# A ternary feed-forward written as a pipeline over tiles, with its weights and first rows made beside the cross-attention ahead of it, and the head of the last attention cut into pieces

## The chip, the cores and the metric

The kernel runs on one core of one Trainium2 chip. Its metric is the time of one execution on the device, in microseconds (us), as a median over runs. A core has five engines with a queue of instructions each: TensorE (PE in the profile, with its weight loads as PEld), VectorE (DVE), ScalarE (ACT), GpSimd (POOL) and SyncE (SP), which here only issues DMAs. Each queue runs in order; queues wait for each other by semaphores.

## What is computed

A decoder of four layers on 16 sequences of 128 tokens with 256 features. Each layer has a mixer (`attn`), a cross-attention (`xattn`) on a context of 16 x 128 tokens with 192 features, and a feed-forward (`ffn`), each on the layer-normed rows and added to `x`. Two of the twelve blocks are rewritten by the change. Layer 1's feed-forward has ternary weights and rows rounded to 8 bits:

```python
def _weight_quant(w):
    scale = 1.0 / jnp.clip(jnp.mean(jnp.abs(w)), 1e-05)
    wq = jnp.clip(jnp.round(w * scale), -1.0, 1.0) / scale
...
def _act_quant(x):
    scale = 127.0 / jnp.clip(jnp.max(jnp.abs(x), axis=-1, keepdims=True), 1e-05)
    xq = jnp.clip(jnp.round(x * scale), -128.0, 127.0) / scale
...
gate = jax.nn.silu(_bitlinear(x, w_gate))
up = _bitlinear(x, w_up)
return _bitlinear(gate * up, w_down)
```

`w_gate` and `w_up` take 256 features to 1024, `w_down` takes them back. Layer 3's attention has 16 heads of 16 features, and each head attends over all 2048 tokens at once:

```python
flat = jnp.transpose(proj.reshape(B, S, H, hd), (2, 0, 1, 3)).reshape(H, B * S, hd)
q = jnp.einsum('hnd,hde->hne', flat, wq)
k = jnp.einsum('hnd,hde->hne', flat, wk)
logits = jnp.einsum('hne,hme->hnm', q, k) / jnp.sqrt(jnp.asarray(D, x.dtype))
attn = jax.nn.softmax(logits, axis=-1)
out = jnp.einsum('hnm,hmd->hnd', attn, flat)
```

## The kernel before

`x` stays on the chip: four groups (NG) of four tiles (GB) of 128 tokens (P), so a group has 512 tokens (GT) and there are 16 tiles (B). The blocks follow each other; a scheduler orders what is written in the program on each engine, by what is ready and within the buffers of the pools, except for TensorE instructions written as `pinned`, which keep their written order among themselves. Weights are fetched by `self.load` into a ring of seven large buffers (tag `w8`), so that a load is issued on SP's queue when an earlier weight's last reader is done.

*Cross-attention* (`xattn64`, L919). It is written as a pipeline over 32 units in layer 1: unit m is four head pairs of one tile of tokens. In each unit TensorE makes the sums of the unit before, scores, values of the unit before, the exponentials' shift, the row maxima of the unit after, and the projection of two units before. VectorE makes a reciprocal `r`, the product `cT`, the negated maxima `nm` and the addition to `x`. Once in four units a `prologue` makes keys, queries and values for the next four, evacuated by VectorE.

*Ternary feed-forward* (`l1_ffn`, L1099). VectorE first takes the absolute sums of the three weights (128 x 2048 each), then scales and clips them (L1122, L1123) and converts them to bf16 -1, 0, 1 (L1125). Then, group by group: layernorm and row rounding, both on GpSimd (L205, L1095), transposes `hTb`; and, tile by tile in halves of 512 columns: `gu` (gate and up together in PSUM, L166), Silu on ACT into `gy` (L1146), a scaled copy `up` on ACT (L1148), their product on GpSimd (L1149); then per tile the maximum (L1090), scale and rounding (L1095) on VectorE, `dy` on GpSimd (L1152), eight transposes `ytr` (L1158), `yT` on ACT (L1159), eight matmuls `down`, and the addition to `x` (L1165). Rounding is by adding and taking away a large constant, MAGIC.

*Last attention* (`l3_attn`). All matmul operands are split into bf16 parts that are summed in one matmul of 113 rows. The head makes, for each group, projections (`project`), the token-major values (`by_token`), and for each half of the features the parts of queries and keys (`split`), made by turns on ACT (L1886, L1892), POOL (L1889, L1893) and DVE (L1891), and written to memory; `fetch` brings them back, arranged by rows, as `qp` and `kp`. Row 112 of `qp` holds each query's negated maximum: `maxima` is a generator that makes one pair of score matmuls (`one`) and two reductions (L1978) at a time, 16 pairs for two heads and a group of queries; `some(n)` makes n pairs; `shift()` transposes finished maxima and sends them through memory into row 112 by two DMAs on POOL's queue (`shifts<-shift`, then `qp<-shifts`). The loop then runs 264 steps, each with two score matmul pairs `st`, exponentials (L2101), values `acc`, and two pairs of maxima for what comes later. In every 32nd step the fetches for a following window are issued, all at once:

```python
w, o = divmod(s - 8, 2 * B)
if o == 0 and 1 <= w and w + 1 < 8:
    queries(w + 1)
    if w % 2 == 0 and w // 2 + 1 < 4:
        keys(w // 2 + 1)
```

Of the kernel before, what the change touches and what calls it, by code (L numbers as in the profile page):

```python
# [8 lines left out]
F = mybir.dt.float32  # L9
BF = mybir.dt.bfloat16  # L10
U32 = mybir.dt.uint32
AF = mybir.ActivationFunctionType
ALU = mybir.AluOpType
# [16 lines left out]
class Decoder:  # L30
# [888 lines left out]
    def xattn64(self, H, names, bias, tag):  # L919
# [5 lines left out]
        wq, wo = self.load(names[0]), self.load(names[3])  # L925
        wk_, wv = self.load(names[1]), self.load(names[2])
        for w, n in ((wk_, names[1]), (wv, names[2])):
            nc.sync.dma_start(out=w[64:P, 1, :], in_=self.a[n][P:DC, :])
        R = lambda j: slice(64 * j, 64 * j + 64)
        S = lambda t: slice(t * P, (t + 1) * P)  # L930
        units = [(g, n, t) for g in range(NG) for n in range(H // 8) for t in range(GB)]
        with self.tc.tile_pool(name=tag, bufs=1) as wk:
# [132 lines left out]
            for m in range(N + 2):  # L1065
# [14 lines left out]
                if m < N and t == GB - 2 and m + 2 < N:  # L1080
                    state[(m + 2) // GB] = prologue(*units[m + 2][:2])

    def l1_xattn(self):
        self.xattn64(16, [f"L1_xattn_{n}" for n in ("Wq", "Wk", "Wv", "Wo")], "L1_xattn_bo", "l1x")

    def quantized(self, src, out, unit, engine):

        nc = self.nc
        nt = src.shape[1]
        nc.vector.tensor_reduce(unit, src, AX.X, ALU.max, apply_absolute_value=True)  # L1090
        nc.vector.tensor_scalar(unit, unit, 1e-5, 1.0 / 127.0, ALU.max, ALU.mult)
        q = self.small([P, nt], "qscale")
        nc.vector.reciprocal(q, unit)
        for t in range(nt):
            engine.tensor_scalar(out[:, t, :], src[:, t, :], q[:, t : t + 1], MAGIC, ALU.mult, ALU.add)  # L1095

    def l1_ffn(self):

        nc = self.nc  # L1099
        ws = [self.load(f"L1_ffn_{n}") for n in ("w_gate", "w_up", "w_down")]  # L1100
        with self.tc.tile_pool(name="l1f", bufs=1) as wk:

            mean = wk.tile([P, 3], F, tag="mean", name="mean")
            part = wk.tile([P, 3], F, tag="part", name="part")
            wsc = wk.tile([P, 3], F, tag="wsc", name="wsc")
            shift = wk.tile([P, 1], F, tag="shift", name="shift")
            nc.gpsimd.memset(shift, -MAGIC)
            for i, w in enumerate(ws):
                flat = w.rearrange("p c n -> p (c n)")
                p16 = self.small([P, 16], "p16")  # L1110
                nc.vector.tensor_reduce(
                    p16, flat.rearrange("p (a n) -> p a n", a=16), AX.X, ALU.add, apply_absolute_value=True
                )
                nc.vector.tensor_reduce(part[:, i : i + 1], p16, AX.X, ALU.add)
            ps = self.b1("wsum")[:, 0:3]
            self.mm(ps, [(self.ones, part)])
            nc.vector.tensor_scalar(mean, ps, 1.0 / (1024 * DM), 1e-5, ALU.mult, ALU.max)
            nc.vector.reciprocal(wsc, mean)
            wb = []
            for i, w in enumerate(ws):  # L1120
                flat = w.rearrange("p c n -> p (c n)")
                nc.vector.tensor_scalar(flat, flat, wsc[:, i : i + 1], 1.0, ALU.mult, ALU.min)  # L1122
                nc.vector.tensor_scalar(flat, flat, -1.0, MAGIC, ALU.max, ALU.add)  # L1123
                t = wk.tile(list(w.shape), BF, tag=f"wb{i}", name=f"wb{i}")
                nc.vector.tensor_scalar(t.rearrange("p c n -> p (c n)"), flat, -MAGIC, None, ALU.add)  # L1125
                wb.append(t)
            wg, wu, wd = wb
            for g in range(NG):
                h = self.layernorm(g, nc.gpsimd)
                ds = self.small([P, GB], "ds")  # L1130
                self.quantized(h, h, ds, nc.gpsimd)
                hT = wk.tile([P, 2, GT], BF, tag="hTb", name="hTb", bufs=2)
                self.transpose_group(h, hT, shift=-MAGIC)
                sg = self.small([P, 2, GB], "sg")
                for i in range(2):
                    nc.vector.tensor_scalar(sg[:, i, :], ds, mean[:, i : i + 1], None, ALU.mult)
                for t in range(GB):
                    y = wk.tile([P, 1, 1024], F, tag="gy", name="gy", bufs=3)
                    for n in range(2):
                        o = slice(n * 512, (n + 1) * 512)  # L1140
                        ps = self.b2("gu")
                        for i, w in enumerate((wg, wu)):
                            self.mm(
                                ps[:, i * 512 : (i + 1) * 512], [(hT[:, k, t * P : (t + 1) * P], w[:, k, o]) for k in range(2)]
                            )
                        nc.scalar.activation(y[:, 0, o], ps[:, 0:512], AF.Silu, scale=sg[:, 0, t : t + 1])  # L1146
                        up = wk.tile([P, 512], F, tag="up", name="up", bufs=2)
                        nc.scalar.activation(up, ps[:, 512:1024], AF.Copy, scale=sg[:, 1, t : t + 1])  # L1148
                        nc.gpsimd.tensor_tensor(y[:, 0, o], y[:, 0, o], up, ALU.mult)  # L1149
                    dy = self.small([P, 1], "dy")  # L1150
                    self.quantized(y, y, dy, nc.vector)
                    nc.gpsimd.tensor_scalar(dy, dy, mean[:, 2:3], None, ALU.mult)  # L1152
                    yT = wk.tile([P, 8, P], BF, tag="yT", name="yT", bufs=2)
                    for n in range(2):
                        ps = self.b1("ytr")
                        for k in range(4):
                            o = (4 * n + k) * P
                            nc.tensor.transpose(ps[:, k * P : (k + 1) * P], y[:, 0, o : o + P], self.ident)  # L1158
                        nc.scalar.activation(  # L1159
                            yT[:, 4 * n : 4 * n + 4, :].rearrange("p c n -> p (c n)"), ps, AF.Identity, bias=shift  # L1160
                        )
                    po = self.b1("down")[:, 0:DM]
                    self.mm(po, [(yT[:, k, :], wd[:, k, :]) for k in range(8)])
                    xt = self.x[g][:, t, :]
                    nc.vector.scalar_tensor_tensor(xt, po, dy[:, 0:1], xt, ALU.mult, ALU.add)  # L1165
# [647 lines left out]
    def l3_attn(self):  # L1813
# [40 lines left out]
        with self.tc.tile_pool(name="l3a", bufs=1) as wk:  # L1854
# [22 lines left out]
            def split(g, half):  # L1877

                ps = two("qk")
                for i in range(2):  # L1880
                    pinned(ps[:, i, :], wqk[:, i, half, :], pT[half][:, G(g)], start=True, stop=True)
                room = es[(g + half) % 3]
# [11 lines left out]
                for n in range(3):  # L1894
# [4 lines left out]
                    )  # L1899

            def transposed(g):
# [7 lines left out]
                return hT  # L1909

            def project(g, hT):
                ps = two("pT")
                for half in range(2):
# [4 lines left out]
                    )  # L1918

            def by_token(g):  # L1920
                for half in range(2):
# [5 lines left out]
                    )  # L1927

            def fetch(i, hg, dst, lo, n, want):

                for b in range(7):
                    j = 0
                    while j < 4:
                        m = j + 1
                        if want(b, j):
                            s = orders[j][i][b]
                            while m < 4 and want(b, m) and orders[m][i][b] == s:
                                m += 1
                            src = parts[s, i, (4 * hg + j) * 16 : (4 * hg + m) * 16, lo : lo + n]
                            moved(  # L1940
                                nc.sync, out=dst[16 * b : 16 * b + 16, j:m, :], in_=src.rearrange("(j r) n -> r j n", r=16)
                            )
                        j = m

# [5 lines left out]
            def queries(w, want=every):  # L1950

                fetch(0, w // 2, qp[w % 2], w % 2 * 2 * GT, 2 * GT, want)

            def keys(hg, want=every):
                fetch(1, hg, kp[hg % 2], 0, T, want)
# [55 lines left out]
            hT = transposed(0)  # L2011
            for g in range(NG):
                project(g, hT)
                if g + 1 < NG:
                    hT = transposed(g + 1)
                split(g, 0)
                by_token(g)
                if g < 2:
                    fetch(0, 0, qp[0][:, :, G(g)], g * GT, GT, first)
                fetch(1, 0, kp[0][:, :, G(g)], g * GT, GT, first)  # L2020
                if g > 0:
                    some(4)
                    fetch(1, 0, kp[0][:, :, G(g - 1)], (g - 1) * GT, GT, front)
                if g == 1:
                    fetch(0, 0, qp[0][:, :, G(0)], 0, GT, front)
            fetch(1, 0, kp[0][:, :, G(3)], 3 * GT, GT, front)
            split(0, 1)
            some(2)
            keys(0, back)
            split(1, 1)  # L2030
            some(2)
            fetch(0, 0, qp[0][:, :, G(1)], GT, GT, front)
            queries(0, back)
            split(2, 1)
            shift()
            some(3)
            split(3, 1)
            some(7)
            queries(1)
            keys(1)  # L2040

            def values(work):
# [243 lines left out]
```

## Time and profile before

| what | us |
|---|---|
| median of 3 runs | 3717.78 |
| their lowest and highest | 3717.32 and 3721.62 |
| profiled execution | 3721.63 |
| its span | 3719.9 |
| layer 1's cross-attention, in the span | about 1268 to 1639 |
| layer 1's feed-forward | about 1637.5 to 1769 |
| head of layer 3's attention | about 2551 to 2637.6 |
| its loop | 2637.6 to about 3380 |

The span runs from the first to the last instruction; the 1.7 us around it belong to the execution. A busy time counts an engine's instructions, not its waits. "PEclk" in the page and in the tables of stretches is the clock that TensorE was granted, as a share of full speed; over the whole span it was 0.941. Row by row, a group of instructions shows line, engine, operation, output and inputs, shapes and count, then the busy time and the mean of one in ns, then the idle time of that engine just ahead, with what ended it.

### The profile page before, as it was taken

Reading aid. Unit: us, or ns where it says so; the run is one execution under the profiler, and the core shown is the slowest. Engines: PE = TensorE matmul, PEld = TensorE weight load, DVE = VectorE, ACT = ScalarE, POOL = GpSimd, SP = SyncE. Lnnn points to the kernel's source line nnn. Section 1 sums busy time; section 2 is a strip of 40 time slices with the busy share of each in tenths; the row PEclk is TensorE's granted clock in tenths of the full one; section 3 lists DMA queues with packets and bytes.
Section 4 is the critical chain, followed back from the end, with each engine's and each line's share of the span. In section 5 each row is a group of like instructions: output and inputs, shape, how many; then the busy total and the mean of one; then the engine's idle time right before and its main releaser. Section 6 shows DMA issues by size and latency. Waiting matters only on the chain.

```text
span 3719.9 us, 51499 instructions
## 1 busy us (share of the span) xinstructions
PE 3379.5 (91%) x20976; PEld 1816.7 (49%) x20976; DVE 2095.8 (56%) x4102; ACT 1433.7 (39%) x1951; POOL 537.3 (14%) x690
## 2 busy tenths in 40 slices
PE   7888999999998899986799999386899999999999
PEld 4555655555556566653355556253122222224665
DVE  5545444444554444455577744424798999973440
ACT  2344311111124322236455522022476777774221
POOL 5423000000003211135000020102200000002100
PEclk9988999999999999998899999597799999999989
DMA  3000000000010100010000000282512020000000
GB/s 96 6 5 5 13 18 22 17 22 17 27 47 2 37 1 1 1 46 1 13 1 1 14 1 7 86 286 67 104 22 31 11 31 11 11 1 25 1 8 17
DMA packets 90486, 105.47 MB, mean 28 GB/s; under 512 B 11364, under 2 KB 72679, under 8 KB 89991
## 3 DMA queue, kind: packets, MB, share of 16 engines
q1 hardware_dynamic: 79672, 89.71, 9.3%
q0 software_dynamic: 4224, 6.43, 0.5%
q10 hardware_dynamic: 6352, 6.03, 0.5%
q8 instruction: 165, 2.70, 0.3%
q14 instruction: 73, 0.59, 0.1%
HBM read 85.53 MB, written 16.60 MB: 27 GB/s over the span
## 4 chain that ended last, share of the span: by engine, by line
PE 80%; DVE 9%; ACT 4%; POOL 3%; issue 3%; DMA 1%; SPq 0%; POOLq 0%; ACTq 0%; DVEq 0%
PE acc L1846 7%; PE down L255 6%; PE gate L255 6%; PE up L255 6%; PE st L1846 6%; PE proj L255 6%; PE one L1846 4%; PE st L255 4%; PE qT L166 3%; PE o L255 2%; PE h L255 2%; PE rb L255 2%; PE v L948 2%; PE pr L166 2%; PE kT L948 2%
## 5 line engine op out<-in xcount | busy, mean ns | idle before, releaser
L1978 DVE TENSOR_REDUCE mx<-one 128x1 f32<-128x512 f32 x1024 | 659.9, 686 | 54.1 <-PE one L1846 43.7
L2101 ACT ACTIVATE e<-st 128x1024 f32<-128x1024 f32 x512 | 496.9, 1021 | 210.8 <-PE st L1846 209.6
L674 ACT ACTIVATE gs<-gate,cols 128x512 f32<-128x512 f32 x132 | 90.8, 688 | 552.8 <-PE gate L255 552.7
L1846 PE MATMUL acc<-e,v 128*32 128x512 f32 x2048 | 290.5, 619 | 1.7 <-ACT e L2101 1.7
L1846 PE MATMUL st<-qp,kp 113*128 113x512 bf16 x1024 | 275.1, 389 | 10.0 <-ACT e L2101 5.7
L688 DVE SCALAR_TENSOR_TENSOR x<-down,w_all,x 128x256 f32<-128x256 f32 x512 | 212.3, 477 | 111.1 <-PE down L255 110.9
L255 PE MATMUL down<-expert,gs 128*128 128x256 f32 x1056 | 250.9, 381 | 2.2 <-DVE gs L675 2.2
L255 PE MATMUL gate<-hT,expert 128*128 128x512 f32 x528 | 250.3, 597 | 0.0
L255 PE MATMUL up<-hT,expert 128*128 128x512 f32 x528 | 248.8, 593 | 0.0
L255 PEld LDWEIGHTS down<-expert,gs 128*128 128x128 f32 x1056 | 201.4, 191 | 86.0 <-issue 61.5
L1846 PE MATMUL one<-kp,qp 16*128 16x512 bf16 x1024 | 224.5, 395 | 13.2 <-DVE mx L1978 7.5
L675 DVE SCALAR_TENSOR_TENSOR gs<-up,cols,gs 128x512 f32<-128x512 f32 x132 | 99.0, 750 | 230.1 <-PE up L255 230.0
L1846 PEld LDWEIGHTS <-qp 16*128 16x128 bf16 x1024 | 49.4, 91 | 333.9 <-issue 330.3
L255 PEld LDWEIGHTS up<-hT,expert 128*128 128x128 f32 x528 | 100.8, 191 | 127.2 <-issue 127.0
L1846 PEld LDWEIGHTS <-kp 113*128 113x128 bf16 x1024 | 79.4, 98 | 149.7 <-issue 87.9
L1050 DVE TENSOR_TENSOR cT<-o,rb 128x512 f32<-128x512 f32 x64 | 44.3, 692 | 165.2 <-ACT rb L1048 165.2
L1048 ACT COPY rb<-rb 128x512 f32<-128x512 f32 x64 | 37.5, 586 | 252.6 <-PE rb L255 252.6
L255 PEld LDWEIGHTS gate<-hT,expert 128*128 128x128 f32 x528 | 100.4, 192 | 70.5 <-issue 64.1
L166 PE MATMUL qT<-hT,L_xattn_Wq 128*128 128x512 f32 x256 | 116.4, 608 | 8.6 <-DVE hT L110 4.4
L1249 DVE SCALAR_TENSOR_TENSOR xs<-xBC,cols,xs 128x508 f32<-128x508 f32 x144 | 106.1, 741 | 22.2 <-ACT xs L1245 18.8
L255 PE MATMUL o<-e,v 128*32 128x128 f32 (+1 forms) x2048 | 105.7, 280 | 11.8 <-DVE nm L292 11.8
L780 POOL MEMSET v<- 128x256 f32 x16 | 5.4, 346 | 680.3 <-DVE bnmv L202 636.6
(516 smaller groups left out, 5643.0 us busy)
## 6 DMA issues: line engine op xcount, KB each, us to landing
W<-in_L_ffn_W_dram SPq DMA_DIRECT2D x46, 512.0 KB, 5.3
expert<-in_L_ffn_Wg_dram SPq DMA_DIRECT2D x32, 128.0 KB, 2.2
expert<-in_L_ffn_Wu_dram SPq DMA_DIRECT2D x32, 128.0 KB, 2.4
expert<-in_L_ffn_Wd_dram SPq DMA_DIRECT2D x32, 128.0 KB, 2.4
parts<-parts SPq DMA_DIRECT2D x16, 256.0 KB, 3.4
qp<-parts SPq DMA_DIRECT2D x28, 128.0 KB, 4.3
kp<-parts SPq DMA_DIRECT2D x12, 256.0 KB, 7.8
hs<-zero SPq DMA_DIRECT2D x23, 128.0 KB, 1.9
```

What stands on the lines that cost most here:

```text
L166: self.nc.tensor.matmul(out, lhsT, rhs, start=i == 0, stop=i == n - 1 and bias is None)
L255: self.tc.keep_in_program_order(self.nc.tensor.matmul(*a, **k))
L674: nc.scalar.activation(gs, pg, AF.Silu, bias=bg)
L675: nc.vector.scalar_tensor_tensor(gs, pu, bu, gs, ALU.add, ALU.mult)
L688: nc.vector.scalar_tensor_tensor(xt, pd[:, t, :], w_all[:, o : o + 1], xt, ALU.mult, ALU.add)
L948: nc.tensor.matmul(ps, l, r, start=True, stop=False)
L1048: nc.scalar.copy(rb, ps)
L1050: nc.vector.tensor_tensor(cT, po, rb, ALU.mult)
L1249: stt = lambda *a: pin(nc.vector.scalar_tensor_tensor(*a))
L1846: self.tc.keep_in_program_order(nc.tensor.matmul(*a, **k))
L1978: nc.vector.tensor_reduce(mx[:, t, kc, i : i + 1], pair[i], AX.X, ALU.max)
L2101: nc.scalar.activation(e[:, 2 * p : 2 * p + 2, :], ps, AF.Exp, scale=1.0 / 16.0)
```

## The change

1. `xattn64` takes a `begin` function; layer 1's hands back pieces of work by unit, which are written behind that unit's own work: absolute sums of the three weights at units 10 to 12, means at 13, scaling at 14 to 16, rounding at 17 to 19, layernorm statistics of groups 0 and 1 at 23 and of group 2 at 27, rounded rows at 24, 25 and 29, transposes at 27, 28 and 31, conversion to bf16 at 28 into buffers of the ring `w8`. All rows are made on VectorE. The order of weight loads changes to Wq, Wk, Wv, Wo in the cross-attentions of layers 1 to 3 that use `xattn64`.
2. `l1_ffn` is a loop over tiles with all TensorE instructions pinned: in step s the gate product of tile s, `down` of tile s - 3, the up product of tile s, the transposes of tile s - 2. Silu and the rounding run over 1024 columns at once on ACT, gate times up is one VectorE instruction that reads PSUM, and `dy` alone remains on GpSimd. Statistics, rows and transposes of group 3 stand in steps 1, 3 and 5.
3. In the head of the last attention the pieces of `split`, `project`, `transposed` and `by_token` are generators with a pair of maxima between them; `shift()` stands behind `split(1, 1)` rather than `split(2, 1)`; 27 pairs stand ahead of the loop rather than 26.
4. In its loop fetches are collected in a list and issued two in each step.

The functions that it replaces are printed above; the diff is cut to what is new.

```diff
-    def xattn64(self, H, names, bias, tag):
+    def xattn64(self, H, names, bias, tag, begin=None):
...
-        wq, wo = self.load(names[0]), self.load(names[3])
-        wk_, wv = self.load(names[1]), self.load(names[2])
+        wq, wk_, wv, wo = (self.load(n) for n in names)
         for w, n in ((wk_, names[1]), (wv, names[2])):
             nc.sync.dma_start(out=w[64:P, 1, :], in_=self.a[n][P:DC, :])
+        beside = begin() if begin else {}
...
+                for work in beside.get(m, ()):
+                    work()
...
+        self.xattn64(16, [f"L1_xattn_{n}" for n in ("Wq", "Wk", "Wv", "Wo")], "L1_xattn_bo", "l1x", self.l1_ffn_begin)
...
-    def l1_ffn(self):
...
+    def l1_ffn_begin(self):
...
+        def scaled(i):
+            nc.vector.tensor_scalar(flats[i], flats[i], wsc[:, i : i + 1], 1.0, ALU.mult, ALU.min)
+        def rounded(i):
+            nc.vector.tensor_scalar(flats[i], flats[i], -1.0, MAGIC, ALU.max, ALU.add)
+        def ternary():
+            t = self.wp.tile([P, 4, 1024], BF, tag="w8", name="gu8", bufs=7)
+            u = self.wp.tile([P, 8, DM], BF, tag="w8", name="down8", bufs=7)
+            st["w"] = t[:, 0:2, :], t[:, 2:4, :], u
+            for w, flat in zip(st["w"], flats):
+                nc.vector.tensor_scalar(w.rearrange("p c n -> p (c n)"), flat, -MAGIC, None, ALU.add)
...
+        def rows(g):
+            mv, rs = hs[g]
+            h = self.hp.tile([P, GB, DM], F, tag="h", name="h", bufs=2)
+            for t in range(GB):
+                nc.vector.tensor_scalar(
+                    h[:, t, :], self.x[g][:, t, :], mv[:, t, 0:1], rs[:, t : t + 1], ALU.subtract, ALU.mult
+                )
+            ds = self.small([P, GB], "l1ds")
+            q = self.scale8(h, ds, "l1q")
+            for t in range(GB):
+                nc.vector.tensor_scalar(h[:, t, :], h[:, t, :], q[:, t : t + 1], MAGIC, ALU.mult, ALU.add)
+            sg = self.small([P, 2, GB], "l1sg")
+            for i in range(2):
+                nc.vector.tensor_scalar(sg[:, i, :], ds, mean[:, i : i + 1], None, ALU.mult)
+            st["sg"][g] = sg
+            hs[g] = h
+        def turn(g):
+            if g % 2 == 0:
+                st["hT"].append(self.hp.tile([P, 2, 2, GT], BF, tag="hT", name="hTb", bufs=5))
+            for k in range(2):
+                ps = self.b1("tr")
+                for t in range(GB):
+                    self.pinned_transpose(ps[:, t * P : (t + 1) * P], hs[g][:, t, k * P : (k + 1) * P])
+                nc.vector.tensor_scalar(st["hT"][g // 2][:, g % 2, k, :], ps, -MAGIC, None, ALU.add)
+        st["last"] = [lambda: stats([3]), lambda: rows(3), lambda: turn(3)]
+        at = lambda f, *a: lambda: f(*a)
+        return {
+            10: [at(absolute, 0)],
+            11: [at(absolute, 1)],
+            12: [at(absolute, 2)],
+            13: [means],
+            **{14 + i: [at(scaled, i)] for i in range(3)},
+            **{17 + i: [at(rounded, i)] for i in range(3)},
+            23: [at(stats, [0, 1])],
+            24: [at(rows, 0)],
+            25: [at(rows, 1)],
+            27: [at(stats, [2]), at(turn, 0)],
+            28: [ternary, at(turn, 1)],
+            29: [at(rows, 2)],
+            31: [at(turn, 2)],
+        }
...
+    def l1_ffn(self):
...
+            def product(w, s):
+                g, t = divmod(s, GB)
+                ps = self.b2("gu")
+                hT = f["hT"][g // 2][:, g % 2]
+                for n in range(2):
+                    o = slice(n * 512, (n + 1) * 512)
+                    for k in range(2):
+                        self.pinned(ps[:, o], hT[:, k, t * P : (t + 1) * P], w[:, k, o], start=k == 0, stop=k == 1)
+                return ps
+            def gated(s, ps):
+                y = wk.tile([P, 1, 1024], F, tag="gy", name="gy", bufs=4)
+                nc.scalar.activation(y[:, 0, :], ps, AF.Silu, scale=f["sg"][s // GB][:, 0, s % GB : s % GB + 1])
+                return y
+            def quantized(s, y, ps):
+                sg = f["sg"][s // GB][:, 1, s % GB : s % GB + 1]
+                nc.vector.scalar_tensor_tensor(y[:, 0, :], ps, sg, y[:, 0, :], ALU.mult, ALU.mult)
+                dy = self.small([P, 1], "dy")
+                q = self.scale8(y, dy, "qy")
+                nc.gpsimd.tensor_scalar(dy, dy, f["mean"][:, 2:3], None, ALU.mult)
+                return dy, q
+            def turned(y):
+                yT = wk.tile([P, 8, P], BF, tag="yT", name="yT", bufs=3)
+                for n in range(2):
+                    ps = self.b1("ytr")
+                    for k in range(4):
+                        o = (4 * n + k) * P
+                        self.pinned_transpose(ps[:, k * P : (k + 1) * P], y[:, 0, o : o + P])
+                    nc.scalar.activation(
+                        yT[:, 4 * n : 4 * n + 4, :].rearrange("p c n -> p (c n)"), ps, AF.Identity, bias=f["down"]
+                    )
+                return yT
+            def down(s, yT, dy):
+                ps = self.b1("down")[:, 0:DM]
+                for k in range(8):
+                    self.pinned(ps, yT[:, k, :], wd[:, k, :], start=k == 0, stop=k == 7)
+                xt = self.x[s // GB][:, s % GB, :]
+                nc.vector.scalar_tensor_tensor(xt, ps, dy[:, 0:1], xt, ALU.mult, ALU.add)
+            ys, dys, yTs = {}, {}, {}
+            for s in range(B + 3):
+                if s < B:
+                    y = gated(s, product(wg, s))
+                if 0 < s <= B:
+                    z = ys[s - 1]
+                    nc.scalar.activation(z[:, 0, :], z[:, 0, :], AF.Identity, scale=qs, bias=f["up"])
+                if s > 2:
+                    down(s - 3, yTs.pop(s - 3), dys.pop(s - 3))
+                if s < B:
+                    ys[s] = y
+                    dys[s], qs = quantized(s, y, product(wu, s))
+                if 1 < s < B + 2:
+                    yTs[s - 2] = turned(ys.pop(s - 2))
+                if s in (1, 3, 5):
+                    f["last"][s // 2]()
...
                     pinned(ps[:, i, :], wqk[:, i, half, :], pT[half][:, G(g)], start=True, stop=True)
+                    if i == 0:
+                        yield
...
+            def issue(moves, n=99):
+                for out, in_ in moves[0:n]:
+                    moved(nc.sync, out=out, in_=in_)
+                del moves[0:n]
...
-            hT = transposed(0)
...
-            split(2, 1)
+            def first_keys(g):
+                issue(fetch(1, 0, kp[0][:, :, G(g)], g * GT, GT, first))
+            def run(pieces, pairs=0):
+                for _ in pieces:
+                    some(min(pairs, 1))
+            run(transposed(0))
+            for g in range(2):
+                run(project(g))
+                run(transposed(g + 1))
+                run(split(g, 0))
+                run(by_token(g))
+                issue(fetch(0, 0, qp[0][:, :, G(g)], g * GT, GT, first))
+                first_keys(g)
+            run(project(2), 1)
+            issue(fetch(1, 0, kp[0][:, :, G(0)], 0, GT, front))
+            run(transposed(3), 1)
+            run(split(2, 0), 1)
+            first_keys(2)
+            issue(fetch(0, 0, qp[0][:, :, G(0)], 0, GT, front))
+            run(by_token(2))
+            run(project(3), 1)
+            issue(fetch(1, 0, kp[0][:, :, G(1)], GT, GT, front))
+            run(split(3, 0), 1)
+            first_keys(3)
+            run(by_token(3), 1)
+            for g in (2, 3):
+                issue(fetch(1, 0, kp[0][:, :, G(g)], g * GT, GT, front))
+            run(split(0, 1), 1)
+            some(1)
+            issue(keys(0, back))
+            run(split(1, 1), 1)
+            issue(fetch(0, 0, qp[0][:, :, G(1)], GT, GT, front))
             shift()
-            some(3)
-            split(3, 1)
-            some(7)
-            queries(1)
-            keys(1)
+            some(1)
+            issue(queries(0, back))
+            run(split(2, 1), 1)
+            some(1)
+            run(split(3, 1), 1)
+            some(5)
+            waiting = queries(1) + keys(1)
...
-                    queries(w + 1)
+                    waiting += queries(w + 1)
                     if w % 2 == 0 and w // 2 + 1 < 4:
-                        keys(w // 2 + 1)
+                        waiting += keys(w // 2 + 1)
+                issue(waiting, 2)
```

## The prediction

> **What bounds the kernel now.** I read the totals and slices of the page first, then tables of busy time by stage, then the costliest groups, waits and chain inside the two stages that the change rewrites.
>
> ```profile
> PE 3379.5 (91%) x20976; PEld 1816.7 (49%) x20976; DVE 2095.8 (56%) x4102; ACT 1433.7 (39%) x1951; POOL 537.3 (14%) x690
> PE   7888999999998899986799999386899999999999
> PEclk9988999999999999998899999597799999999989
> ...
> 1522.00:1568.00 46.00, 45.47 (x376) 28.61 (x375) 19.34 (x31) 9.98 (x15) 11.29 (x16) 1.00 0.00 1
> ...
> 1640.00:1655.00 15.00, 5.03 (x18) 2.10 (x19) 14.68 (x21) 1.40 (x2) 12.12 (x4) 0.58 0.48 158
> 1655.00:1768.00 113.00, 76.14 (x401) 44.88 (x400) 63.43 (x150) 73.72 (x118) 61.55 (x60) 0.86 0.00 1
> ```
>
> TensorE is full nearly everywhere, so only its thin places can pay. Columns of the windows: stretch, its length, busy PE, PEld, DVE, ACT, POOL, granted clock, DMA share, GB/s. In the cross-attention (1522 to 1568) PE is 99% busy and DVE 42%. The ternary feed-forward (1637.5 to 1769, 131.5 us) begins with 15 us in which PE waits for VectorE to make the weights, then no engine is over 67% in 113 us: a chain passing from engine to engine.
>
> ```profile
> L1149 POOL TENSOR_TENSOR gy<-gy,up 128x512 f32<-128x512 f32 x32 | 40.8, 1292 | 22.8 <-ACT up L1148 19.8 <-PE down L166 3.0
> L1090 DVE TENSOR_REDUCE dy<-gy 128x1 f32<-128x1024 f32 x16 | 19.5, 1219 | 24.4 <-POOL gy L1149 24.4
> L205 POOL TENSOR_SCALAR h<-x,bnmv,rstd 128x256 f32<-128x256 f32 x8 | 17.0, 2134 | 6.6 <-PE tr L183 6.6
> ```
>
> The chain is GpSimd's: `gy` then `dy`, on one queue. `h` on the same queue adds whole blocks (the chain of waits shows one of 4.88 us at 1681.47).
>
> The last attention's head (2551 to 2637.6) is thin as well:
>
> ```profile
> 2592.00:2609.00 17.00, 14.25 (x30) 5.45 (x30) 6.48 (x11) 4.41 (x6) 3.97 (x5) 0.70 0.37 113
> 2609.00:2638.00 29.00, 22.24 (x48) 5.33 (x48) 18.76 (x32) 11.82 (x13) 18.82 (x12) 0.74 0.72 181
> ...
> 2862.68 0.53 POOL L1852 DMA_DIRECT2D qp<-shifts  x1 [8.13 <-PE st L1846]
> 2866.89 1.04 PE L1846 MATMUL st<-qp,kp 113*128 113x512 bf16 x4 [2.27 <-DMA qp<-shifts]
> ...
> 2850.00:2860.00 10.00, 9.99 (x62) 2.45 (x55) 9.43 (x16) 6.95 (x9) 0.53 (x1) 1.00 0.98 123
> 2870.00:2880.00 10.00, 10.00 (x40) 2.18 (x36) 5.56 (x10) 4.46 (x5) 0.46 (x1) 0.50 0.00 0
> ```
>
> In its last 46 us PE runs at 0.70 to 0.74 and nobody is full; in the loop, a burst of SP's fetches (DMA share 0.98) makes `qp<-shifts` late, PE stops for 2.27 us, and the clock is halved after it.
>
> **What the Trainium skill says.** "TensorE: Matmul & The Clock Gate", Part 1, gives half clock after an idle window of about 3.4 us and full clock after about as much steady work. The trace agrees on the halving, not on sizes: a 2.27 us gap sufficed, and these small matmuls stayed at 0.50 from 2867 to about 2885. "Trainium Kernel Development and Optimization", Key Constraints: DMAs of all issuing queues run on the same 16 engines and interleave. The trace agrees: the row of shifts lands in 1.6 us at the median and took up to 9.1. "GPSIMD Engine Reference", section 3.1, says a two-input elementwise pass is about twice as slow there as on VectorE; here 128x512 takes 1292 ns on POOL, and a gate-like pass from PSUM (`gs`, L675) 750 ns on DVE.
>
> **The change, part by part.**
>
> *Weights and first rows of the ternary layer, beside L1's cross-attention.* Removed from the feed-forward's start: six DVE passes, three conversions, layernorm, rows and transposes of group 0. By the chain from 1639.35 to 1656.5 that is 17 us before the first product group is running; afterwards the first product needs only its LDWEIGHTS and a Silu, say 3 us. Added beside the cross-attention: 9 weight passes at about 1.2 us (11), 12 layernorm statistics at 0.60 (7), rows of three groups at 4.6 (14), six evacuations of `hTb` at 0.68 (4): 36 us of DVE, in the last 18 of the 32 units of 6.48 us, of which DVE has 58% or 3.8 us free each, 68 us in all. PE gets 24 transposes more, at 0.13 warm: 3 us, moved and not new. So capacity hides it; order may not. DVE is a queue: reciprocal `r`, `cT` and the negated maxima `nm` stand behind the inserted passes, and PE's `values` and `exponentials` wait for these. In the new order at most three weight passes stand in a row, 3.7 us, about the slack. The tight place is the last prologue: the three conversions, then the scalings of L2's four input weights. Their DMAs are moved: `L_f_wz` and `L_f_wx` take the buffers that the conversions free, `L_b_wz` and `L_b_wx` those of Wq and Wv, so SP issues them only there (`L_b_wx` was issued at 1639.3 before), and each scaling waits some 4 us for its load with evacuations, `r` and `nm` behind it. I count 5 us lost (bounds: 0 if the evacuations were never urgent; 20 if such stalls halve the clock for three units, which then take about 11 us instead of 6.48, 13.5 us, and the stalls themselves take 6). The sqrt for the statistics needs the table of the activation engine twice more in the cross-attention: two pairs of 1.28 us loads on an ACT that is 22% busy; nothing.
>
> *The feed-forward as a pipeline.* Per tile, POOL keeps only `dy`. DVE: gate times up over 128x1024 from PSUM (twice 128x512 at 750 ns less one fixed part: 1.28), reduce 1.22, two small 0.31, `x` 0.48, semaphores and turnaround 0.6: 3.9. PE: 8 products 1.7, 8 transposes 1.06, `down` 1.1: 3.85 warm. ACT: Silu 128x1024 1.05, the quantising pass 1.05 (taken from `exp` of that size, 1.02), two `yT` at 0.64: 3.4. Everything is issued one to three tiles ahead of its use, so the step is the busiest engine plus hand-overs: I take 4.2, times 16 = 67. Unhidden: statistics, rows and transposes of group 3 and L2's first tokens on DVE, about 15, since DVE bounds the step; start 3; three draining steps 6. Sum 91. Against 131.5 this gains 40 (bounds 22 to 48: steps of 5.3 if ACT and DVE wait for each other, 3.9 and half of the extras hidden).
>
> *Order of weight loads in L2's and L3's cross-attention.* Loads land far ahead of use; nothing, with the same work covering them.
>
> *Head of the last attention.* `split`, `project`, `by_token` become pieces with a pair of maxima after each: 27 pairs before the loop rather than 26, so at 1.37 us a pair DVE gets 1.4 us more work there, removed from the loop. `shift()` moves from after `split(2,1)` to after `split(1,1)`. It issues two DMAs on POOL's queue, and they pass two `e`/`parts` operations of 2.13 us each on it; before, `shifts` went out at 2630.4 and `qp<-shifts` at 2633.0, the last thing the loop waited for. What is late next is PE itself: from 2592 to 2638 it was busy 36.5 of 46 us at clock 0.70 to 0.74. At the same clock the floor is 37 us (gain 9); warm it is 36.5 x 0.72 = 26 (gain 20). I take 14 (bounds 0, if the turns between ACT and POOL, 8 x 3.2 = 26 us from 2606, still end last, to 20).
>
> *The loop's fetches, two per step.* They were bursts of 12 to 26 on SP's queue. Spread out, `shifts` and `qp<-shifts` find free DMA engines. The stall at 2864.6 goes (2.3), its half clock too: from 2866.9 on four steps took about 5.0 for 2.6, so 9.6; the stall at 3050 (1.6) also. Sum 13.5; I take 12 (bounds 0 to 14, below nothing only if the fetches become late: 26 at two per step are out after 13 steps, and the first use lies some 18 after their issue begins).
>
> Sum: -40 + 5 - 14 - 12 = -61. The profiled execution took 3721.63 (span 3719.9, and 1.7 around it); it would take 3661. The median of the runs shown lies 3.9 lower, 3717.78, so **3657** by the median.
>
> **The rivals.**
>
> *A, lock-step (0.17).* ACT's quantising pass waits for DVE's scale of the same tile, DVE's next product waits for Silu behind it on ACT. If they alternate, a step is ACT's 2.1 plus DVE's 3.4, 5.5 us: 88 + 24 = 112, a gain of 19. With the rest 3678. For: the tightest loop of waits in the new order. Against: Silu of the next tile is queued ahead of the quantising pass.
>
> *B, the head and loop don't move (0.15).* ACT and POOL still take turns (the waits show 45.1 us of POOL waiting for ACT there) and the DMA share of 0.72 stays: -35 only, 3683. For: the page of waits. Against: the shifts were plainly last, and the burst is gone by construction.
>
> *C, all better (0.15).* Loop entered warm (2640 to 2660 ran at 0.50, so 10 saved), no loss beside the cross-attention: 3641.
>
> *D, slower (0.06).* DVE's queue stalls PE for over 2 us in the cross-attention's insertions and the clock stays at half: a unit of 6.48 then takes about 11. The gain of 66 without the 5 charged above is gone after 15 such units (4.5 each); with all 18 that carry inserted work it is 81, and the time 3718 + 15 = 3733. For: the gate reacts to 2.3 us, and this is the one stage where work is put in front of a full PE. Against: only two or three insertions exceed the slack, and full-size matmuls keep PE busy between.
>
> *E, no change (0.02):* the new steps are bound like the old, and the head too, 3715.
>
> **How the numbers follow.** The forecast has 0.45, own range 3648 to 3668. A and B widen the top to 3690, C the bottom to 3632; outside are D, E and small tails, under 2 in 10. A measurement here tells apart about 0.2%, 7.4 us: faster is forecast, A, B, C and a little of nothing else, 0.92; same 0.02; slower 0.06.
>
> **What would show it.** The stage between the last `proj` and L2's first product should last about 91, with POOL nearly idle and DVE over 90%; its first 15 us no longer PE-empty. Units of the cross-attention should stay at 6.5 with clock 1.00 but for the last five. The first `st` of the loop should come about 70 us after the head begins (86.6 before), and no half-clock stretch follow the second window. Wrong I am if PE waits for `nm`, `r` or `cT` over several units, if ACT idles for `qy` in every step, or if POOL's `parts` still ends the head.

## The result, and the profile after

| | us |
|---|---|
| before, median of 4 runs | 3717.55 (3715.1 to 3721.62) |
| after, median of 4 runs | 3656.47 (3647.31 to 3659.25) |
| ratio | 0.983, 95% interval 0.981 to 0.9851 |
| profiled execution after | 3659.25, span 3657.5 |

The forecast was 3657. The sum was right, several of its terms were not. Read from the first and last instructions of each stage (first `kT` of layer 1's cross-attention, first and last `st` of a stage, last `proj`, first `xBC` of L2, first `pT` of the last attention), the two profiled executions differ by

| stage | before | after | change | predicted |
|---|---|---|---|---|
| up to L1's cross-attention | 1268.3 | 1266.8 | -1.5 | 0 |
| its first prologue | 26.4 | 23.7 | -2.7 | 0 |
| its units, first `st` to last `proj` | 344.3 | 346.4 | +2.1 | +5 |
| last `proj` to L2's first `xBC` | 131.5 | 79.4 | -52.1 | -40 |
| L2, to the first `pT` | 781.0 | 781.6 | +0.6 | 0 |
| head of the last attention | 86.2 | 74.9 | -11.3 | -14 |
| its loop, first `st` to last | 738.7 | 741.2 | +2.5 | -12 |
| the rest | 343.6 | 343.5 | -0.1 | 0 |
| span | 3719.9 | 3657.5 | -62.4 | -61 |

So 12 us more came out of the ternary layer than forecast, and 14 us less out of the loop. Each column is one execution, and not every row repeats: the first row lies within the spread of later executions (the changed kernel and its variants reach this point after 1261 to 1271 us), the head and the loop are taken up below. The page after, totals and two rows of slices:

```profile
PE 3343.9 (91%) x20959; PEld 1806.8 (49%) x20976; DVE 2115.8 (58%) x4133; ACT 1426.7 (39%) x1917; POOL 457.2 (12%) x627
...
PE   7888999999998899997799999196999999999999
...
PEclk9978999999999999999999999597799999999989
```

POOL's busy time fell by 80 us, DVE's rose by 20. The ternary layer after, as stretches (length, busy PE, PEld, DVE, ACT, POOL, clock, DMA share, GB/s):

```profile
1637.00:1655.00 18.00, 13.35 (x64) 6.93 (x63) 14.88 (x31) 14.12 (x15) 1.14 (x3) 0.91 0.19 59
1655.00:1705.00 50.00, 43.47 (x283) 28.44 (x288) 47.29 (x103) 48.53 (x60) 3.60 (x12) 1.00 0.01 1
```

The 15 us in which PE had waited for weights are gone, and in the 50 us after them ACT is 97% busy, DVE 95%, PE 87%: a chain has become a balanced pipeline. Its costliest groups on ACT and DVE (busy us, mean ns, then idle time ahead):

```profile
L1222 DVE SCALAR_TENSOR_TENSOR gy<-gu,l1sg,gy 128x1024 f32<-128x1024 f32 x16 | 20.4, 1278 | 3.1 <-ACT gy L1217 2.8 <-PE gu L255 0.3
L1235 ACT ACTIVATE yT<-ytr,l1f 128x512 bf16<-128x512 f32 x32 | 20.3, 682 | 2.0 <-PE ytr L258 2.0
L1253 ACT ACTIVATE gy<-gy,l1f,qy 128x1024 f32<-128x1024 f32 x16 | 19.8, 1240 | 0.5 <-DVE qy L1094 0.4
L1091 DVE TENSOR_REDUCE dy<-gy 128x1 f32<-128x1024 f32 x16 | 19.4, 1214 | 0.1
L1217 ACT ACTIVATE gy<-gu,l1sg 128x1024 f32<-128x1024 f32 x16 | 17.9, 1117 | 1.5 <-PE gu L255 1.4
L1217 ACT ACT_TABLE_LOAD x5 | 6.4, 1283 | 3.8 <-DVE bnst L1146 3.8
L191 ACT ACT_TABLE_LOAD x5 | 6.4, 1283 | 0.1
```

Nobody waits long here. ACT's 58 us of passes and its loads of tables (sets of values for its functions, 11 loads here with one at L1289) fill the layer.

In the last attention the clock tells the story (columns as above; the loop's first `st` stands at 2572.8):

```profile
2532.80:2542.80 10.00, 8.66 (x27) 2.99 (x26) 7.78 (x12) 3.55 (x5) 3.90 (x5) 0.82 0.66 199
2552.80:2562.80 10.00, 9.39 (x17) 2.03 (x17) 5.25 (x9) 3.34 (x6) 6.89 (x4) 0.50 1.00 200
2582.80:2592.80 10.00, 9.96 (x26) 1.34 (x26) 5.80 (x10) 2.05 (x2) 0.50 (x1) 0.50 1.07 128
2592.80:2602.80 10.00, 10.00 (x28) 1.47 (x28) 6.81 (x11) 2.88 (x3) 0.00 (x0) 0.50 0.27 30
2612.80:2622.80 10.00, 9.37 (x61) 2.44 (x61) 9.17 (x16) 6.56 (x8) 1.01 (x2) 1.00 0.01 2
```

From about 2539 to 2611 PE ran at half clock (0.50), 38 us of it in the loop, though it was 100% busy for the last 25. Before, the loop was entered at half clock too, but for 25 us. How much of this difference belongs to the change is asked below.

### The profile page after: what moved, and what is told of

It is laid out like the page before. It is cut to its first block, busy times and chain, and to the rows that moved or that the text cites. A ratio compares the mean times of both kernels' runs of the same rounds, so it can differ in the third digit from the quotient of the medians.

```text
span 3657.5 us, 51423 instructions
## 1 busy us (share of the span) xinstructions
PE 3343.9 (91%) x20959; PEld 1806.8 (49%) x20976; DVE 2115.8 (58%) x4133; ACT 1426.7 (39%) x1917; POOL 457.2 (12%) x627
## 4 chain that ended last, share of the span: by engine, by line
PE 79%; DVE 10%; ACT 5%; issue 3%; POOL 2%; DMA 1%; SPq 0%; POOLq 0%; ACTq 0%; DVEq 0%
PE acc L1943 7%; PE down L255 6%; PE gate L255 6%; PE up L255 6%; PE proj L255 6%; PE st L1943 5%; PE one L1943 4%; PE qT L166 4%; PE st L255 4%; PE o L255 2%; PE h L255 2%; DVE mx L2089 2%; PE rb L255 2%; PE v L948 2%; PE pr L166 2%
## 5 line engine op out<-in xcount | busy, mean ns | idle before, releaser
L1943 PE MATMUL one<-kp,qp 16*128 16x512 bf16 x1024 | 211.7, 399 | 4.0 <-DVE mx L2089 2.6
L962 POOL CAST kb<-kT 128x512 bf16<-128x512 f32 x64 | 41.5, 677 | 433.9 <-DVE kT L110 433.9
```

The costliest lines, as they stand in the source:

```text
L962: nc.gpsimd.tensor_copy(kb[:, i + j, :], kT[:, i + j, :])
L1943: self.tc.keep_in_program_order(nc.tensor.matmul(*a, **k))
```

## The experiments

Times are medians in us; where a run of the changed kernel stands beside it, the stage lengths of the profiled executions decide, since the whole varies by some 10 us from run to run (the last experiment says why).

**1. Each half alone.** The first kernel has the change in `xattn64` and `l1_ffn` and keeps `l3_attn` as it was before; the second has the change in `l3_attn` and keeps all else as it was.

> The kernel before with the ternary layer's part of the change alone (hook in the cross-attention, weights and rows beside it, pipeline over tiles). Theory: all of the 52 us between the last proj and L2's first product come from this part and nothing of them is taken back later: 3665, the feed-forward 79 us, the last attention as before (head 86, loop 739). Rival, that a part of it is taken back in L2 because its input weights are now loaded later: 3670 to 3680 with waits for L_b_wx after the feed-forward.

> The kernel before with the last attention's part of the change alone (head in pieces, shift earlier, two fetches per step). Theory: head 11 us shorter, loop 2 longer (stall at the second window gone, but entered at half clock for some 35 us): about 3708. Rival, that the loop's first stretch at half clock is chance and not made by this head: half clock at the loop's start for 20 us as before, and about 3696.

Layer 1's part: 3658.36, ratio 0.9856 (0.983 to 0.9882). Ternary layer from its first product to `xBC` 79.4 (79.0 in the changed kernel), L2 779.5: nothing of the gain is taken back by weights that are loaded later. Layer 3's part: 3709.91, ratio 0.999 (0.9979 to 1.0001), so no change that can be told from none; head 74.7 (86.2 before), loop 737.4, entered at half clock for 27 us, between the theory's 35 and the rival's 20. Nearly the whole gain is the ternary layer's. A surprise is in the first: its loop and head are the ones of before, and yet its loop took 733.8, not 738.7, and its head 82.2, not 86.2. Head and loop together took 816.0 there and 816.1 in the changed kernel, so most of the 8.8 us by which they are shorter in the table may belong to the one execution of before. The stall at the second window, on which a term of the prediction rested, isn't there:

```profile
2790.60:2795.60 5.00, 5.00 (x33) 1.22 (x32) 4.97 (x8) 3.88 (x4) 0.14 (x1) 1.00 1.08 130
2795.60:2800.60 5.00, 5.00 (x32) 1.23 (x32) 4.94 (x9) 3.70 (x4) 0.51 (x1) 1.00 0.45 55
```

The same burst of fetches (DMA share 1.08) goes by with PE full and the clock at 1.00. This is one execution, as is the one with the stall.

**2. The loop's fetches in one go.**

```diff
-                issue(waiting, 2)
+                issue(waiting)
```

> The changed kernel, but the loop issues all waiting fetches at once. Theory: the burst makes the row of shifts late at the second window, PE stops over 2 us, half clock follows there for some 17 us: 11 us slower than the changed kernel, about 3667. Rival, that the stall came from where shift stood and spreading the fetches gives nothing: 3654 to 3659, clock 1.00 through the second window.

Measured 3653.81 (3646.76 to 3657.73), ratio 0.9834 (0.9809 to 0.9859); second window at clock 1.00. The theory falls, and further than the rival said: in the last attention the queues of all five engines hold the same instructions in the same order with the same waits, with two per step or all at once. SP has nothing else to do in the loop, so where in the program a fetch is written doesn't hold it back; only its data and buffers do. In the changed kernel itself, SP's queue at the second window:

```profile
2784.10 4.97 SPq L1949 DMA_DIRECT2D qp<-parts  x11
2789.12 10.24 SPq L1949 DMA_DIRECT2D kp<-parts  x14
```

25 fetches in 15 us are a burst still; before, the same 25 took 15 us too (from 2840.8 to 2856.0). This run is thus the changed kernel once more, and its loop took 734.7 where that took 741.2: half clock at the entrance for 17 us rather than 38.

**3. An even number of pairs ahead of the loop.** In the changed kernel TensorE waits for VectorE at the end of nearly every one of the 32 groups of maxima; the timeline of one such place (start, length, engine, what, idle before and releaser):

```profile
2702.32 1.29 DVE L2089 TENSOR_REDUCE mx<-one 128x1 f32<-128x512 f32 x2
...
2703.64 0.19 DVE L2093 TENSOR_REDUCE mn<-mx 128x8 f32<-128x32 f32 x1
...
2703.88 0.27 PE L1946 MATMUL one<-ident,mn 128*8 128x128 f32 x1 [0.63 <-DVE mn L2093]
```

With 27 pairs ahead, the 16th pair of a group is the first of a step, and `shift()` in the same step transposes what VectorE has just begun to reduce.

```diff
-            some(5)
+            some(6)        # pairs28; some(4) in pairs26
             waiting = queries(1) + keys(1)
```

> The changed kernel with 28 pairs of maxima ahead of the loop instead of 27. Theory: with an odd number the 16th pair of a group falls on the first of a step's two pairs, and shift, which follows in the same step, makes TensorE wait for VectorE's last maxima (31 waits of 0.66 us); with an even number it falls on the second pair, shift comes a step later and the waits go: a step of the loop takes 2.75 instead of 2.79 us, the loop is 10 us shorter and the head about 1.4 longer, 8 to 9 less in all. Rival, that VectorE bounds the loop and the waits cost nothing: the step stays at 2.79.

> The changed kernel with 26 pairs ahead of the loop, as before the change. Theory: as with 28, steps of 2.75 us and no waits for mn; the head 1.4 us shorter than with 27. Rival: steps of 2.79 us, since the pieces and not the number of pairs made the difference.

Measured 3650.91 with 28 (ratio 0.9824, 0.9796 to 0.9853) and 3657.74 with 26 (one run). TensorE's waits for VectorE between 2620 and 3250 (total us, times, longest), with 27 pairs:

```profile
PE one L1946 <- DVE mn L2093: 18.4, 28, 0.8
PE one L1946 <- DVE mx L2089: 4.8, 27, 0.2
```

and with 28, where no wait for `mn` is left:

```profile
PE one L1946 <- DVE mx L2089: 4.9, 27, 0.2
```

In 400 us at full clock the loop makes 286 exponentials, two a step, with 27 pairs and 291 with 26 or 28: 2.79 and 2.75 us a step, 10 us over the loop, so about half of the 18 us of waits cost time. The theory holds in both. The loop took 732.9 with 28 pairs, entered at half clock for 33 us, and 735.8 with 26, entered so for 45 us.

**4. What holds the clock.** Dense matmuls that nothing reads, first only ahead of the loop:

```diff
             waiting = queries(1) + keys(1)
+            for _ in range(12):
+                pinned(acc, self.identb, dense, start=True, stop=True)
```

> The changed kernel with 12 dense matmuls (128 rows, 128 columns, 512 elements, bf16) into the idle bank of acc right ahead of the loop; nothing reads them. Theory: the loop's first 37 us run at half clock because the head ends in matmuls of 16 rows, which don't bring the clock back; the dense ones cost about 5 us and bring it back, so the loop starts at full clock and gains 15 to 18: about 3645. Rival, that the clock comes back after a fixed time whatever runs: 5 us slower, 3661.

Measured 3657.85 (3641.72 to 3665.95): not told apart from the changed kernel. By stages, head 79.5 for 74.9, loop 729.4 for 741.2, so 7 us net. The clock came back at the end of the twelve and fell again in the loop's first steps (0.63 in 2580.9 to 2590.9), so the theory was half right: in this execution the clock came back with the dense work, and what followed did not keep it. Next, with 28 pairs, throughout the head's end and the loop's entrance:

```diff
                 for _ in pieces:
                     some(min(pairs, 1))
+                    dense(2 * pairs)
...
-            some(5)
+            for _ in range(6):
+                some(1)
+                dense(1)       # dense2: 2
...
+                if s < 16:                                  # dense2: 12
+                    dense(1, ones[(turn[0] + 1) % 3])       # dense2: 2
                 some(1)
```

> The changed kernel with 28 pairs ahead and dense matmuls (128 rows, 128 columns, 512 elements, bf16; nothing reads them): two after each piece of the head that has a pair, one after each of the last six pairs, one in each of the loop's first 16 steps. Theory: the clock falls in the head because PE then runs matmuls of 16 rows with gaps under 0.8 us, and dense matmuls hold it: half clock in the head's last 35 us and the loop's first 37 us is gone or under 10 us; they cost 0.22 us each warm, about 10 us, and bring 25, so 15 less than with 28 pairs alone. Rival, that the clock falls for another reason (gaps alone): half clock as before and 10 to 20 us slower.

> As the kernel with dense matmuls, with two instead of one after each of the last six pairs of the head, and two in each of the loop's first 12 steps instead of one in 16. Theory: in that kernel the clock fell 5 us ahead of the loop, where one dense matmul of 0.22 us stands against four of 16 rows, so it is the share of full-height work that holds the clock: with two it stays at 1.00 through the entrance, head and loop together 4 to 8 us shorter than with one, about 3640. Rival, the clock falls by the gaps: half clock as with one, and 3 to 5 us slower for the added work.

One each: 3645.95 (ratio 0.9814, 0.9793 to 0.9836), head 70.2, loop 729.3. After its first 4 us the head stayed at 1.00 up to 5 us ahead of the loop, where one dense matmul stands against two of 16 rows. Head and loop are 9.5 us shorter than with 28 pairs alone, where 15 was expected. Two each: 3641.04 (0.9804, 0.9778 to 0.9831), head 70.8, loop 727.8, together 1 us shorter than with one each and not 4 to 8: of the half clock from the head's end through the loop's entrance some 7 us are left for 24, but the added matmuls take time themselves. Its stretches around the first `st` at 2566.7:

```profile
2546.70:2556.70 10.00, 8.78 (x30) 2.46 (x29) 8.29 (x15) 5.88 (x7) 7.68 (x6) 1.00 0.56 147
2556.70:2566.70 10.00, 9.85 (x32) 1.86 (x32) 8.70 (x15) 3.92 (x4) 6.85 (x5) 0.89 0.76 164
2566.70:2576.70 10.00, 8.77 (x31) 1.56 (x29) 7.64 (x13) 4.38 (x5) 2.61 (x2) 0.84 0.94 236
2576.70:2586.70 10.00, 9.85 (x39) 1.82 (x38) 7.24 (x12) 3.07 (x3) 0.50 (x1) 0.93 1.09 125
```

PE is no busier than in the changed kernel (8.8 to 9.9 of 10 us), and the clock is 0.84 to 1.00 where it was 0.50. More matmuls, and a faster stage. The head is at half clock for 4 to 9 us in the three executions with dense matmuls throughout, and for 30 to 43 in the eleven others. Gaps alone don't explain the low clock, since the changed kernel stayed at 0.50 with PE 100% busy. How the dense matmuls hold it (by the gaps that they fill, or by their rows, columns or kind of data) wasn't separated.

**5. What bounds the ternary layer now.**

```diff
# pool_round
-                    nc.scalar.activation(z[:, 0, :], z[:, 0, :], AF.Identity, scale=qs, bias=f["up"])
+                    nc.gpsimd.tensor_scalar(z[:, 0, :], z[:, 0, :], qs[:, 0:1], MAGIC, ALU.mult, ALU.add)
# act_more
+                    if s > 1:
+                        nc.scalar.activation(spare, ys[s - 1][:, 0, 0:512], AF.Identity)
```

> The changed kernel with the rounding of the gated rows on GpSimd instead of ScalarE. It takes 16 passes of 1.24 us, 20 us, from ScalarE and gives GpSimd 16 passes of about 1.9 us. Theory: ScalarE (97% busy, its loads of tables included) sets the ternary layer's step now, VectorE (95%) is just behind: the layer goes from 79 to 73 to 76 us. Rival, that VectorE or the chain of hand-overs sets it: 79 or more.

> The changed kernel with one more pass of 128x512 on ScalarE in 15 of the 16 steps, whose output nothing reads: 15 x 0.65 = 10 us. Theory, ScalarE sets the step: the ternary layer takes 10 us more, 88 to 90. Rival, VectorE sets it: at most 3 us more.

Rounding on GpSimd: first product to `xBC` 75.7 for 79.0, as the theory has it (3653.09, one run); with the best kernel below that makes two executions at 75.6 and 75.7, against 78.7 to 79.8 in ten with the rounding on ScalarE. The pass takes less there than on ScalarE, not more:

```profile
L1253 POOL TENSOR_SCALAR gy<-gy,qy 128x1024 f32<-128x1024 f32 x16 | 18.1, 1131 | 0.0
```

More work on ACT: 79.4, no longer, as the rival has it, but not for its reason (3654.42, one run). ACT stayed full; the scheduler put something else out:

```profile
L1256 ACT ACTIVATE spare<-gy 128x512 f32<-128x512 f32 x15 | 9.5, 631 | 0.0
L1217 ACT ACT_TABLE_LOAD x3 | 3.8, 1283 | 3.8 <-DVE bnst L1146 3.8
L191 ACT ACT_TABLE_LOAD x3 | 3.8, 1283 | 0.1
L1340 ACT ACTIVATE h<-h,ss 128x256 f32<-128x256 f32 x4 | 1.8, 498 | 0.0
```

Of the changed kernel's five and five loads and eight `h`, four loads and four `h` have left: 5.1 + 2.1 us of L2's first rows, moved behind the layer, where they cost nothing (L2 778.9). What I had counted as unhidden work is filler that goes where there is room. What the layer takes with the loads of tables alone removed has no measurement.

**6. All that helped, and the changed kernel beside it.** The best kernel is the one with two dense matmuls each, with the rounding on GpSimd too.

> The changed kernel with the three things that helped by themselves: 28 pairs of maxima ahead of the loop, two dense matmuls per piece and pair at the head's end and in the loop's first 12 steps, and the rounding of the gated rows on GpSimd. Theory: the stages are apart and their gains add: ternary layer 75.7 instead of 79, head and loop about 17 us shorter than in the changed kernel: 3636 to 3640. Rival, that L2's first work, which filled the ternary layer, comes later and takes the 3 us back: 3641 as without it.

> The changed kernel once more, beside the one above on the same chip: 3650 to 3660, with the half clock at the loop's entrance of a length that differs from run to run.

Measured 3637.41 (3632.66 to 3640.71), ratio 0.979 (0.9777 to 0.9804); the changed kernel on the same chip 3661.38 (3661.12 to 3667.18), ratio 0.986 (0.9845 to 0.9875): 24 us better. Ternary layer 75.6, L2 781.8, head 69.5, loop 726.8, so the gains add. The changed kernel has by now been measured three times as the same program, 3656.47, 3653.81 and 3661.38; of the 8 us between its shortest and longest profiled execution (spans 3652.0 and 3659.7) 7 are the loop's, 734.7 and 741.8, entered at half clock for 17 and for 38 us. What sets that length is open: with the head and loop of before it was 25 us in one execution and 33 in the other.

## Why the prediction was right, and where it was not

*The ternary layer, 91 for 79.4.* The mechanism held: POOL out of the chain, work ahead hidden, steps of the busiest engine. From the first `gy` to the last, 15 steps took 64.5 us, 4.30 each, against 4.2 forecast. The term that was mis-sized is "Unhidden: statistics, rows and transposes of group 3 and L2's first tokens on DVE, about 15". DVE's own work is 3.28 a tile (20.4 + 19.4 + 2.4 + 2.5 + 7.7 us over 16), not 3.9: I had put 0.6 of turnaround on every tile and then charged the 15 once more, while 16 x 3.28 + 15 = 67 is about what 16 steps of 4.30 took with both in them. I had also taken ACT for idle at 3.4 a tile: the rounding pass took 1.24, not 1.05, and 11 loads of tables add 14 us. The Trainium skill prices such a load ("ScalarE: Activation LUTs", What ACT_TABLE_LOAD costs: about 1283 ns, and about 1380 of drain on top). The trace has the 1283 to the nanosecond; the drain doesn't show as idle time (0.1 us ahead of L191's five, and the pass behind a load starts within 0.02 us of its end). The two errors had opposite signs, the first the larger.

*Beside the cross-attention, +5 for +2.1.* The tight place is where it was expected. VectorE's queue waits for L2's weights, 2.9 and 2.2 us where some 4 were forecast:

```profile
1594.18 1.16 DVE L1287 TENSOR_SCALAR L_f_wx<-L_f_wx,cols 128x776 f32<-128x776 f32 x2 [2.89 <-DMA L_f_wx<-in_L_f_wx_dram]
...
1600.36 1.16 DVE L1287 TENSOR_SCALAR L_b_wx<-L_b_wx,cols 128x776 f32<-128x776 f32 x2 [2.17 <-DMA L_b_wx<-in_L_b_wx_dram]
```

PE lost little by it and the clock stayed at 1.00, so rival D never came near. The 2.1 us are steady: 346.3 to 346.5 in twelve profiled executions with this part, 344.2 and 344.3 in two without. So is the shorter first prologue, 21.9 to 23.7 us with this part for 26 without, a gain that the forecast put at nothing. The timeline shows whence it comes. The absolute sums, written for units 10 to 12, were scheduled ahead of the first unit, where they had been before. Before, that of `w_down` stood in VectorE's queue ahead of the evacuation of `hT`: it waited for its load (issued at 1268.95) until 1275.80, and `qT` started at 1279.38. After, the load was issued at 1266.99 and the sum began at 1272.30; PE waited 2.15 us ahead of `qT` instead of 4.19.

*The head, -14 for -11.3.* The shift did leave the end of the chain. What was late next was PE at half clock, as said; the forecast took the middle between "same clock" (9) and "warm" (20), and the clock got worse, not better (0.63 in the head's last 46 us for 0.72). The size is less sure than it looks: the old head took 82.2 in the other execution that has it, and the new one 74.7 to 77.1 in the others without dense matmuls. With dense matmuls it is 69.5 to 70.8, 4 to 5 us under the changed kernel's, their own time included.

*The loop, -12 for +2.5.* This step failed. "Spread out, `shifts` and `qp<-shifts` find free DMA engines": they are not spread out (experiment 2), so here the change doesn't do what it says, a rival that I didn't set up. The stall that was to go was an accident of the one execution profiled before; experiment 1 has the old loop without it. It did go. My estimate of its worth is some 10 us: the waits of 2.3 and 1.6, and 17 us at half clock, which at the rate given below cost 5 to 6 and not the forecast's 9.6. Two things took its place: steps longer by 1.4% because 27 is odd (+10, experiment 3), and 38 instead of 25 us at half clock at the entrance. That second one is some 4 us by the two executions of the changed kernel (6.5 us of loop for 21 us more of half clock) and isn't shown to come from the change, since the same program had 17 in another execution. "27 pairs rather than 26, 1.4 us more work there, removed from the loop" saw the price of a pair and not its place in the step.

That 3657 was hit to the microsecond is thus partly luck: 12 us more from the ternary layer and 14 less from the loop nearly cancelled. By the medians of experiment 1 it is plainer still. Layer 1's part was forecast to gain 35 and gained 55; layer 3's was forecast to gain 26 and gained about 4, which can't be told from none.

## What to carry to other kernels

Where each step issues more than one unit of a generator, check on which of them a group ends, and what reads it in the same step: an odd count cost 10 us here. Before a term is built on a stall, look whether a second execution has it, and before one is built on issuing later, whether anything in that queue holds it back. Elastic work at a stage's border (the next stage's norms) is not to be charged to a pipeline that has room for it.

## What the runs showed of the hardware

TensorE stayed at half clock while it was 100% busy for 25 us (2585 to 2610 in the changed kernel) with matmuls of 16 and 113 rows and of 32 columns. "TensorE: Matmul & The Clock Gate" of the Trainium skill, Part 1, has it return after about 3.4 us of sustained work, and lose it by an idle window; here it was lost at about 2539 with no gap over 0.8 us in the timeline (PE busy 1.89 of 3 us from 2536 to 2539), and mostly held with two dense matmuls of 128 rows per pair. So on this kernel being busy isn't enough. Nor does the mix of matmuls alone decide: from 2611 to 3290 the same steps of the loop ran at 1.00. A one-input pass of 128x1024 took 1131 ns on GpSimd and 1240 on ScalarE, so GpSimd is no worse a place for it.
